# Sums at the chunks' ends: a product with ones in place of stores and loads, in a Mamba and FFN block on one core

## The chip, the cores and the metric

The kernel runs on one core of a Trainium2 chip. The metric is the device time of one execution in microseconds. TensorE (PE) multiplies matrices into PSUM, VectorE (DVE), ScalarE (ACT) and GpSimd (POOL) work elementwise, and SyncE (SP) issues nearly all DMAs. Each engine runs its own queue in order and waits for the others by semaphores.

## The reference

There are 4 sequences of 512 tokens with 256 features. A small modulation gives shifts, scales and gates `sa, ca, ga, sb, cb, gb` for each sequence. Then:

```python
h = _layernorm(x) * (1 + ca) + sa
x = x + ga * attn(h)          # Mamba-like, below
h = _layernorm(x) * (1 + cb) + sb
x = x + gb * ffn(h)           # silu(h W1) * (h W3), Hadamard transform, W2

# attn, with 32 heads of 8 channels and 64 states
xBC, z, A_log = split(u @ W_in.T)
x, Bm, Cm = split(depthwise_conv4(xBC) + conv_b)
a  = -softplus(A_log)                    # one decay a head and token
Lm = exp(segsum(a))                      # decay from token s to token l
M  = einsum('blhn,bshn,bhls->bhls', Cm, Bm, Lm)
y  = einsum('bhls,bshp->blhp', M, x) + D * x
out = (y * silu(z + z_bias)) @ W_out.T
```

The kernel cuts the 512 tokens into 8 chunks of 64 (`Q = 64`, `NC = 8`). Inside a chunk it computes M directly. Between chunks it carries a state for each head; the state is multiplied by the decay of a whole chunk, which is the Exp of the running sum of `a` at the chunk's end. This factor, for each head and chunk, is what the change is about.

## The kernel before

The work is cut into 8 units: two halves `i` of the heads (16 heads each) by four sequences `b`, with all sequences of `i = 0` first. A unit has two quads `m` (index `pp`), and a quad has four steps `k` (pairs of heads), so there are 64 steps. After them come 32 steps of the FFN.

For each step, `project` (L780) makes the channels of B (`pbc`, then `bc`) and of C (`pcc`, then `cc`) by six TensorE products each, and `conv` (L722) finishes them on ACT, DVE and POOL. `prep_l` (L773) makes the decays `l` inside the chunks from a product `pl` whose operands `dl` and `dr` are loaded by `load_d`. `attend` (L790) makes the products `pG` for two steps and multiplies them by `l` on DVE. `turn_b` (L807) transposes `bc`.

For each quad, `states` (L870) makes the chunks' states (`ps`, copied to `st`), `turn_states` (L896) transposes them (`sT`) and runs the scan over the chunks (`sn`) with the factors `dc`, and `inter` (L910) and `intra` (L882) make the outputs `pi` and `py`.

For each sequence, `prologue` (L663) has five parts: layer norm, modulation (`ht`, spilled to DRAM as `htd`), running sums of the decays (parts `p` and full sums `phs`, stored to DRAM as `pd`), the decays to the chunks' ends (`df`), and their transpose (`pw`, `wds`). In `phs` a partition is 32t + h for the quarter t of the tokens and the head h, and the free dimension holds the quarter's 128 tokens, so two chunks' ends. `write_sums` (L717) stores the ends to DRAM as `pend`, in four DMAs. For each unit `x_fetch` (L815) loads `pd` as `ex` and `pend` as `de` (spread over all 128 partitions), and `x_decays` (L827) takes the Exp of `ex`, the Exp of `de` into `dx`, sets the first chunk's factor to zero, and copies it into `dc` (1024 columns for both quads).

The order of the work is planned while the kernel is built. Each call has a time in steps for its writing (table `R`) and a due time in steps (table `T`). `Plan.schedule` (L266) goes through the engines with estimated durations. On an engine it takes, among the operations that it believes ready, the one with the earliest due time, but none whose due time is more than 10 steps after the earliest work left (`WINDOW`). For SP it keeps at most 8 DMAs under way. Buffers of one tag form a ring, ordered by due time, and a tile waits for the release of the tile that many buffers before it. The queues that come out of this are fixed: on the chip each engine waits at each instruction until its inputs are there.

The output weights are loaded in `load_wo` (L564), in two halves, through the ring `stage` of three buffers, which also serves `wm`, the modulation's weights (`load_mod`, L463; used by the products `pm` and `pg`), and projection weights `wq`. DVE scales each half of `wo` by 0.5:

```python
sp.dma_start(st[:, :DM], wo_t[128 * k : 128 * k + 128])
ve.tensor_scalar(st[:, :DM], st[:, :DM], 0.5, None, ALU.mult)
```

Where TensorE would idle for over 300 ns by the plan, up to 60 products of zeros (`zeros<-idle`) fill the time. Nearly all instructions are issued by one line of the planner, L366, so the profile's groups are told apart by their tiles' names.

Of the kernel before, what the change touches and what calls it, by code (L numbers as in the profile page):

```python
# [366 lines left out]


def mamba_ffn(tc, ctx, u, c_t, wmod, win_t, cw, cb, zb, dsk, wo_t, w13_t, w2_t,
              k_ident, k_reset, k_dl, k_dr, k_had, k_own, out):  # L370
    nc = tc.nc
    plan = Plan(slack=SLACK, retile=RETILE, window=WINDOW)
    ve, ac, gp, pe, sp = [Engine(plan, n, e) for n, e in (("DVE", nc.vector), ("ACT", nc.scalar), ("POOL", nc.gpsimd),
# [42 lines left out]
    def cload(src, shape, name, eng=ac):  # L416
        t = const.tile(shape, F32, name=name)
        eng.dma_start(t, src)
        return t
# [22 lines left out]
    warm = const.tile([128, 4], F32, name="warm")  # L442
    ac.activation(warm, neghalf, AF.Tanh)

    idle = const.tile([128, S], BF16, name="idle")
    ve.memset(idle, 0.0)
    zeros = bank(ps_1, [128, S], "zeros", "y")
    for _ in range(FILLERS):
        plan.open = None
        pe.matmul(zeros, idle[:, :128], idle, start=True, stop=True, kind="b512").filler = True  # L450
    plan.open = None
    c_sb = cload(c_t.rearrange("(k p) b -> p k b", p=128), [128, 2, NB], "c_sb")

# [51 lines left out]
        return t  # L505

    wds = const.tile([128, NB, 4, 2, NH], F32, name="wds")
    hzb = const.tile([128, 2], F32, name="hzb")
    xpad = const.tile([128, 2, NC, 4, 32], F32, name="xpad")
    sts = [const.tile([128, NC - 1, 4, 32], F32, name=f"sts{pp}") for pp in range(2)]  # L510
# [3 lines left out]

    dls = [const.tile([94, 8, 128], BF16, name=f"dl{n}") for n in range(2)]
    drs = [const.tile([94, 4, S], BF16, name=f"dr{n}") for n in range(2)]
    kdl = const.tile([94, 128], BF16, name="kdl")
    kdr = const.tile([94, S], BF16, name="kdr")

    def spread_constants(n):  # L520
        ve.tensor_copy(dls[n], kdl.unsqueeze(1).to_broadcast([94, 8, 128]), kind=325)
# [134 lines left out]
        return ts  # L656

    ht, htd, h2d, x2d, ygd = {}, {}, {}, {}, {}
    wdec, p_dr, p_dr3, p_end = {}, {}, {}, {}

    xns, fulls, phss, dfs = {}, {}, {}, {}

    def prologue(b, part, fill=None):  # L663
        if part == 0:
            xns[b] = normalize(b, 0, x_in.pop(b))
        elif part == 1:
            fulls[b], ht[0, b] = modulate(b, 0, xns.pop(b))
            htd[b] = spill(f"htd{b}", ht[0, b])
        elif part == 2:

            full = fulls.pop(b)
            acc = mtile([128, 3, 128], f"pa{b}")
            pa, sums, rest = acc[:, 0], acc[:, 1], acc[:, 2]
            for k in range(2):
                for t in range(4):
                    pe.matmul(pa[32 * t : 32 * t + 32], wa[:, k], full[k][:, 128 * t : 128 * t + 128],
                              start=(k == 0), stop=(k == 1), skip_group_check=True, tile_position=(0, 32 * t), kind="sums")
            e = work([128, 128], f"spe{b}", "spe", 1)
            ac.activation(e, pa, AF.Abs)
            ac.activation(e, e, AF.Exp, scale=-1.0)  # L680
            ac.activation(e, e, AF.Ln, bias=1.0)
            if fill:
                fill()

            ve.scalar_tensor_tensor(pa, pa, 0.0, e, ALU.max, ALU.add)
            ve.tensor_tensor_scan(sums, reset, pa, 0.0, ALU.mult, ALU.subtract)

            parts = work([128, 3, 128], f"parts{b}", "parts", 1, BF16)
            ve.tensor_copy(parts[:, 0], sums)
            ve.tensor_tensor(rest, sums, parts[:, 0], ALU.subtract)  # L690
            ve.tensor_copy(parts[:, 1], rest)
            ve.tensor_tensor(parts[:, 2], rest, parts[:, 1], ALU.subtract)
            phs = phss[b] = work([128, 128], f"phs{b}", "phs", 1)
            ac.activation(phs, sums, AF.Copy)
            p_dr3[b] = dram.tile([NH, 3, S], BF16, name=f"p3{b}")
            p_dr[b] = dram.tile([NH, S], F32, name=f"pd{b}")
            p_end[b] = dram.tile([NH, NC], F32, name=f"pend{b}")
            sp.dma_start(p_dr3[b].rearrange("h r (t l) -> t h r l", t=4), parts, kind=3000)
            after(1, write_sums, b, phs)
        elif part == 3:  # L700

            phs = phss.pop(b)
            df = dfs[b] = work([128, 128], f"df{b}", "df", 1)
            p_c = phs.rearrange("p (c l) -> p c l", l=Q)
            ve.tensor_tensor(df.rearrange("p (c l) -> p c l", l=Q), p_c[:, :, Q - 1 :].to_broadcast([128, 2, Q]),
                             p_c, ALU.subtract, kind=727)
            ac.activation(df, df, AF.Exp)
        else:
            pw = mtile([128, 128], f"pw{b}")
            pe.transpose(pw, dfs.pop(b), ident, kind="turn")  # L710

            wdec[b] = wds[:, b]
            for q in range(2):
                ac.activation(wdec[b][:, :, q], pw.rearrange("p (t h) -> p t h", h=NH), AF.Copy,
                              scale=own[:, 0, 8 * q : 8 * q + 1])

    def write_sums(b, phs):  # L717
        sp.dma_start(p_dr[b].rearrange("h (t l) -> t h l", t=4), phs, kind=4300)
        for t in range(4):
            sp.dma_start(p_end[b][:, 2 * t : 2 * t + 2], phs[32 * t : 32 * t + 32, Q - 1 :: Q], kind=5800)  # L720

    def conv(ps, tl, dst):  # L722
        w = cw_sb[:, tl]
# [21 lines left out]
        one0=-11.83, one1=-7.06, one2=-4.93, one3=-4.48, one4=-3.88,  # L745
    )
    T = dict(
        attend=0.36, turn_b=0.36, prep_l=-0.51, proj_b=-0.63, proj_c=-0.8, load_d=-6.56, states=0.1, intra=0.9,
        turn=2.34, inter=2.64, x_proj=2.37, x0=4.16, x1=8.55, x2=4.65, x3=3.51, gate_z=6.56, fin0=3.05, fin1=4.05,
        fin2=4.15, fin3=6.83, pro0=-9.52, pro1=-6.69, pro2=-4.23, pro3=1.75, pro4=0.64, next_ht=-6.78, pro04=1.42,  # L750
        quads=0.78, xz1=32.52, wo=21.57, mod=20.38, w2=38.38, wf0=61.86, wf1=70.35, wf2=67.94, load_w2=63.65,
        first_h2=59.92, lag=10.06, next_h2=-8.14, load_x=-11.25, spread=1.25, up=3.02, load_out=4.89, out=18.28,
        one0=-9.5, one1=-7.21, one2=-5.05, one3=-1.53, one4=-0.3,
    )

    def where(k):
        i, b = units[k // 8]
        return i, b, (k // 4) % 2, k % 4

    lts, bcs, ccs, bts, exs, des, xcs, xds, dcs, stt, pys, zts = ({} for _ in range(12))  # L760

    def load_d(m):

# [51 lines left out]
    def x_fetch(n):  # L815
        i, b = units[n]
        exs[n] = work([128, S], f"ex{n}", "ex")
        sp.dma_start(exs[n], p_dr[b].apply(lambda r: bass.AP(r.tensor, r.offset + 16 * i * S, [[S, 16], [0, 8], [1, S]]), [128, S]), kind=3600)

        des[n] = work([128, 16, NC], f"de{n}", "de", 1)  # L820
        sp.dma_start(des[n], p_end[b].apply(lambda r: bass.AP(r.tensor, r.offset + 16 * i * NC,
                                                              [[0, 128], [NC, 16], [1, NC]]), [128, 16, NC]), kind=3800)

    def x_part1(n):
        x_decays(n)

    def x_decays(n):  # L827
        ex = exs[n]
        ac.activation(ex, ex, AF.Exp)

        de = work([128, 16, NC], f"dx{n}", "dx", 1)
        ac.activation(de.rearrange("p (a g j) c -> p a g (j c)", a=2, g=4),
                      des.pop(n).rearrange("p (g a j) c -> p a g (j c)", a=2, g=4), AF.Exp)
        ac.activation(de[:, :, 0:1], de[:, :, 0:1], AF.Copy, scale=0.0)
        dc = dcs[n] = work([128, 16, HD, NC], f"dc{n}", "dc", 1)
        ac.activation(dc, de.unsqueeze(2).to_broadcast([128, 16, HD, NC]), AF.Copy)

    def x_proj(n):
        i, b = units[n]
# [30 lines left out]
    def states(m):  # L870
# [8 lines left out]
        stt[m] = work([128, 4, 128], f"st{m}", "st", 1)  # L879
        ac.activation(stt[m], pst, AF.Copy)  # L880

    def intra(m):  # L882
        n, pp = divmod(m, 2)
        if pp == 0:
            pys[n] = bank(ps_1, [128, S], f"py{n}", "y"), bank(ps_1, [128, S], f"pi{n}", "yi")
        py = pys[n][0]
        for c in range(NC):
            for g in range(4):
                l = slice(Q * c, Q * c + Q)
                pe.matmul(py[32 * g : 32 * g + 32, l], xpad[:, pp, c, g], lts[4 * m + g][:, l],  # L890
                          start=(pp == 0 and c == 0), stop=(pp == 1), skip_group_check=True,
                          tile_position=(0, 32 * g), kind="outs")
        for g in range(4):
            lts.pop(4 * m + g)

    def turn_states(m):  # L896
# [3 lines left out]
        for t in range(4):  # L900
            pe.transpose(pt[:, :, :, 2 * t : 2 * t + 2].rearrange("p g (h x) q -> p (g h) q x", h=2), st[:, t], ident, kind="turn")
        sn = work([128, 4, 16, NC], f"sn{m}", "xd", 2)
        ve.tensor_tensor_scan(sn.rearrange("p g x c -> p (g x c)"),
                              dcs[n][:, 8 * pp : 8 * pp + 8].rearrange("p h x c -> p (h x c)"),
                              pt.rearrange("p g x c -> p (g x c)"), 0.0, ALU.mult, ALU.add)
        o = 16 * pp
        gp.tensor_tensor(sts[pp][:, :, :, o : o + 16].rearrange("p c g x -> p g x c"), sn[:, :, :, : NC - 1],
# [95 lines left out]
    zb_sb = cload(zb, [128, 2], "zb_sb", sp)  # L1003
    d_sb = cload(dsk, [128, 2], "d_sb", sp)
    own = cload(k_own, [128, 4, 16], "own", sp)
    q11 = fetch_quad(1, 1)
    had = cload(k_had, [128, 128], "had", sp)
    prologue(0, 0)
# [165 lines left out]
def _constants():  # L1174
# [12 lines left out]
    while had.shape[0] < 128:  # L1187
        had = np.block([[had, had], [had, -had]])

    own = (p // 64)[:, None, None] ^ (np.arange(4) % 2)[None, :, None] == (np.arange(16) // 8)[None, None, :]  # L1190
    return dict(k_own=own.astype(np.float32), k_ident=np.eye(128, dtype=np.float32), k_reset=reset, k_dl=dl, k_dr=dr,
                k_had=(had / 64.0).astype(np.float32))


# [41 lines left out]
```

## Time and profile before

| what | value |
|---|---|
| median of 3 runs | 553.67 us (551.88 to 554.48) |
| profiled execution, own time | 557.63 us |
| its span, first to last instruction | 555.8 us |
| mean granted TensorE clock | 0.99 |
| busy: PE, DVE, ACT, POOL | 535.1, 403.2, 386.8, 328.2 us |
| DMAs of the chunks' ends | 16 stores `pend` (0.2 KB each), 8 loads `de` (64 KB each) |
| `dx<-de` Exp, 128 columns | 8 x 335 ns |
| `dx<-dx` zeroing, 16 columns | 8 x 246 ns |
| `dc<-dx` copy, 1024 columns | 8 x 1075 ns |

The profile is one execution on the hardware. PE is TensorE's products and PEld its weight loads, which overlap them. Products are pipelined and their ends are modelled, so a busy PE is not one at its peak. The granted clock is the share of full speed that TensorE got. In a list of waits "A <- B: 5.4, 2, 4.0" means that A stood idle for B, 5.4 us in total, twice, at most 4.0 us. In the chain of waits each line is a start time, a length and what the chain passed through. An f32 product that isn't in the rounded format `fp32r` shows as two records.

### The profile page before, as it was taken

The numbers are of one execution on the slowest core, as the hardware profiler recorded it, in microseconds if no ns is written. First come the engines' busy times: TensorE is split into PE (matmuls) and PEld (weight loads), VectorE is DVE, ScalarE is ACT, GpSimd is POOL, SyncE is SP. The second block draws the span as 40 slices with busy tenths as digits, with TensorE's granted clock in tenths as the row PEclk, the third lists the DMA queues.
The fourth block names the chain that finished last, engine by engine and source line by source line (L and its number), as shares of the span: only waits on it lengthen the run. The fifth ranks groups of instructions, "written<-read, shape, count | busy, mean of one in ns | idle before, by whom it ended". The sixth has DMA issues, their size and how long they took to land.

```text
span 555.8 us, 16369 instructions
## 1 busy us (share of the span) xinstructions
PE 535.1 (96%) x6885; PEld 427.4 (77%) x6890; DVE 403.2 (73%) x672; ACT 386.8 (70%) x666; POOL 328.2 (59%) x299
## 2 busy tenths in 40 slices
PE   8899999979998999999999999999989999999996
PEld 4666787758776777777787778777868888888886
DVE  6969889957965988896799989878955533324332
ACT  3999899958987899887787896889763333233231
POOL 7774458435734697663587657758966444425243
PEclk8999999989998999999999999999999999999999
DMA  8532201233125234311022803361391240502002
GB/s 233 173 92 68 71 30 50 70 101 111 43 44 165 66 99 126 106 59 18 20 66 66 267 16 78 147 208 40 118 325 63 89 149 4 158 1 85 1 26 88
DMA packets 41792, 51.99 MB, mean 94 GB/s; under 512 B 17942, under 2 KB 29940, under 8 KB 41720
## 3 DMA queue, kind: packets, MB, share of 16 engines
q1 hardware_dynamic: 41448, 50.96, 29.5%
q8 instruction: 54, 0.88, 0.7%
q14 instruction: 18, 0.15, 0.1%
q10 hardware_dynamic: 272, 0.00, 0.0%
HBM read 33.51 MB, written 17.44 MB: 92 GB/s over the span
## 4 chain that ended last, share of the span: by engine, by line
PE 69%; DVE 14%; DMA 7%; ACT 7%; issue 3%; SPq 1%; POOL 0%; ACTq 0%; DVEq 0%; POOLq 0%
PE f L366 16%; PE pbc L366 11%; PE pcc L366 11%; PE pG L366 4%; PE pdy L366 4%; PE pdyi L366 4%; PE bT L366 4%; PE ps L366 2%; DVE bc L366 2%; DMA wo<-wo_t 2%; PE py L366 2%; DVE cc L366 2%; PE pi L366 2%; PE pl L366 2%; PE px L366 2%
## 5 line engine op out<-in xcount | busy, mean ns | idle before, releaser
L366 DVE SCALAR_TENSOR_TENSOR bc<-pbc,cw_sb,bc 128x511 f32<-128x511 f32 (+1 forms) x128 | 95.0, 743 | 19.3 <-ACT cv L366 17.4
L366 DVE SCALAR_TENSOR_TENSOR cc<-pcc,cw_sb,cc 128x511 f32<-128x511 f32 (+1 forms) x128 | 95.0, 742 | 13.4 <-ACT cv L366 11.4
L366 POOL TENSOR_TENSOR cc<-cc,cv 128x509 f32<-128x509 f32 x64 | 69.7, 1088 | 52.2 <-DVE cc L366 38.3
L366 POOL TENSOR_TENSOR bc<-bc,cv 128x509 f32<-128x509 f32 x64 | 71.2, 1112 | 45.2 <-DVE bc L366 23.6
L366 PE MATMUL f<-h,wf 128*128 128x512 f32 x384 | 93.8, 393 | 0.0
L366 PEld LDWEIGHTS f<-h,wf 128*128 128x128 f32 x384 | 69.9, 188 | 13.7 <-issue 0.2
L366 POOL TENSOR_TENSOR fl<-ft,fh 128x512 fp32r<-128x512 f32 x31 | 39.9, 1288 | 61.4 <-ACT fh L366 61.2
L366 DVE SCALAR_TENSOR_TENSOR ft<-ft,f 128x512 f32<-128x512 f32 x32 | 21.9, 686 | 62.7 <-ACT ft L366 62.7
L366 ACT ACTIVATE bc<-pbc,cb_sb,cw_sb 128x512 f32<-128x512 f32 x64 | 50.4, 787 | 10.6 <-PE pbc L366 9.0
L366 ACT ACTIVATE cc<-pcc,cb_sb,cw_sb 128x512 f32<-128x512 f32 x64 | 50.5, 789 | 8.6 <-PE pcc L366 8.3
L366 ACT ACTIVATE fh<-ft 128x512 fp32r<-128x512 f32 x32 | 20.2, 631 | 51.4 <-PE pdyi L366 48.3
L366 PE MATMUL pbc<-ht,wq 128*128 128x512 f32 x192 | 53.0, 412 | 1.0 <-DVE cc L366 1.0
L366 PE MATMUL pcc<-ht,wq 128*128 128x512 f32 x192 | 52.5, 409 | 1.3 <-DVE bc L366 1.0
L366 PE MATMUL pcc<-hr,wq 128*128 128x512 f32 x192 | 52.8, 410 | 0.8 <-DVE bc L366 0.7
L366 PE MATMUL pbc<-hr,wq 128*128 128x512 f32 x192 | 52.2, 407 | 0.0
L366 ACT ACTIVATE bt<-bT 128x512 f32<-128x512 f32 x64 | 38.8, 606 | 12.6 <-PE bT L366 12.6
L366 DVE TENSOR_TENSOR l<-pG,l 128x512 f32<-128x512 f32 x64 | 41.5, 682 | 7.8 <-PE pG L366 7.1
L366 PEld LDWEIGHTS pbc<-ht,wq 128*128 128x128 f32 x192 | 34.5, 189 | 15.9 <-ACT cc L366 4.0
L366 ACT ACTIVATE cv<-pbc,cw_sb 128x512 f32<-128x512 f32 x64 | 44.7, 698 | 1.5 <-PE pbc L366 1.1
L366 ACT ACTIVATE cv<-pcc,cw_sb 128x512 f32<-128x512 f32 x64 | 44.7, 699 | 0.3 <-PE pcc L366 0.3
L366 PEld LDWEIGHTS pcc<-ht,wq 128*128 128x128 f32 x192 | 34.6, 188 | 9.9 <-ACT wq L366 1.5
L366 PE MATMUL bT<-ident,bc 128*128 128x128 f32 x256 | 40.7, 281 | 1.3 <-ACT ht L366 0.6
(145 smaller groups left out, 1137.4 us busy)
## 6 DMA issues: line engine op xcount, KB each, us to landing
wq<-win_t SPq DMA_DIRECT2D x16, 256.0 KB
htd<-ht SPq DMA_DIRECT2D x8, 512.0 KB
hr<-htd SPq DMA_DIRECT2D x8, 512.0 KB
h2d<-ht SPq DMA_DIRECT2D x8, 512.0 KB
h<-h2d SPq DMA_DIRECT2D x8, 512.0 KB
x<-u SPq DMA_DIRECT2D x7, 512.0 KB
ex<-pd SPq DMA_DIRECT2D x8, 256.0 KB
ygd<-yg SPq DMA_DIRECT2D x4, 512.0 KB
```

The costliest lines, as they stand in the source:

```text
L366: getattr(o.engine.real, method)(*map(real, args), **{k: real(v) for k, v in kw.items()})
```

## The change

The stores `pend` and the loads `de` are gone. In part 3 of `prologue` POOL multiplies the ends of `phs` by a constant mask `pick` into `ends`, which has 32 x 4 x 2 = 256 columns: for each head, each quarter and each of its two chunks there is one column, zero but in the one partition that holds that sum. TensorE multiplies `ends` by a 128x128 matrix of ones, so each of the 128 partitions gets all sums (`pn`). ACT takes the Exp of both halves of the heads, one into a buffer `de` for the unit `i = 0`, one into the constant tile `dec` for `i = 1`, and sets the first chunk's factor to zero. The heads are put in order by the mask. The copy `dc` is made by each quad in `states`, with 512 columns, in place of one for each unit in `x_decays`.

Beside this, `idle` has 128 columns and the fillers read its first column repeatedly; `kdl` and `kdr` share a buffer of the ring `yg`; and all due times `T` are new. The table `R` is the same.

```diff
-    idle = const.tile([128, S], BF16, name="idle")
+    idle = const.tile([128, 128], BF16, name="idle")
...
-        pe.matmul(zeros, idle[:, :128], idle, start=True, stop=True, kind="b512").filler = True
+        pe.matmul(zeros, idle, idle[:, :1].to_broadcast([128, S]), start=True, stop=True, kind="b512").filler = True
...
+    dec = const.tile([128, NB, 16, NC], F32, name="dec")
+    ones = const.tile([128, 128], F32, name="ones")
+    gp.memset(ones, 1.0)
...
-    kdl = const.tile([94, 128], BF16, name="kdl")
-    kdr = const.tile([94, S], BF16, name="kdr")
+    kd = work([94, 128 + S], "kd", "yg", 1, BF16)
+    kdl, kdr = kd[:, :128], kd[:, 128:]
...
-            p_end[b] = dram.tile([NH, NC], F32, name=f"pend{b}")
...
             ac.activation(df, df, AF.Exp)
+
+            ends = work([128, 32, 4, 2], f"en{b}", "ends", 1)
+            gp.tensor_tensor(ends, pick.unsqueeze(3).to_broadcast([128, 32, 4, 2]),
+                             p_c[:, :, Q - 1].unsqueeze(1).unsqueeze(1).to_broadcast([128, 32, 4, 2]), ALU.mult)
+            pn = mtile([128, 32, 8], f"pn{b}")
+            pe.matmul(pn, ones, ends.rearrange("p m t q -> p m (t q)"), start=True, stop=True, kind="gate")
+            for i in range(2):
+                d = dea[i, b] = dec[:, b] if i else work([128, 16, NC], f"de{b}", "de")
+                ac.activation(d, pn[:, 16 * i : 16 * i + 16], AF.Exp)
+                ac.activation(d[:, :, 0:1], d[:, :, 0:1], AF.Copy, scale=0.0)
...
         sp.dma_start(p_dr[b].rearrange("h (t l) -> t h l", t=4), phs, kind=4300)
-        for t in range(4):
-            sp.dma_start(p_end[b][:, 2 * t : 2 * t + 2], phs[32 * t : 32 * t + 32, Q - 1 :: Q], kind=5800)
...
     T = dict(
-        attend=0.36, turn_b=0.36, prep_l=-0.51, proj_b=-0.63, proj_c=-0.8, load_d=-6.56, states=0.1, intra=0.9,
-        turn=2.34, inter=2.64, x_proj=2.37, x0=4.16, x1=8.55, x2=4.65, x3=3.51, gate_z=6.56, fin0=3.05, fin1=4.05,
-        fin2=4.15, fin3=6.83, pro0=-9.52, pro1=-6.69, pro2=-4.23, pro3=1.75, pro4=0.64, next_ht=-6.78, pro04=1.42,
-        quads=0.78, xz1=32.52, wo=21.57, mod=20.38, w2=38.38, wf0=61.86, wf1=70.35, wf2=67.94, load_w2=63.65,
-        first_h2=59.92, lag=10.06, next_h2=-8.14, load_x=-11.25, spread=1.25, up=3.02, load_out=4.89, out=18.28,
-        one0=-9.5, one1=-7.21, one2=-5.05, one3=-1.53, one4=-0.3,
+        attend=0.32, turn_b=0.44, prep_l=-0.48, proj_b=-0.53, proj_c=-0.94, load_d=-5.82, states=0.2, intra=0.97,
+        turn=2.11, inter=2.32, x_proj=2.63, x0=3.34, x1=9.64, x2=2.66, x3=3.55, gate_z=6.9, fin0=3.24, fin1=3.64,
+        fin2=3.85, fin3=7.01, pro0=-9.53, pro1=-8.16, pro2=-4.2, pro3=-1.53, pro4=1.54, next_ht=-7.04, pro04=1.83,
+        quads=-0.67, xz1=30.69, wo=18.7, mod=19.5, w2=38.55, wf0=56.92, wf1=67.73, wf2=63.44, load_w2=64.98,
+        first_h2=59.85, lag=6.12, next_h2=-5.77, load_x=-6.16, spread=5.23, up=2.87, load_out=11.33, out=15.94,
+        one0=-7.18, one1=-6.04, one2=-4.13, one3=0.26, one4=-0.05,
     )
...
-        des[n] = work([128, 16, NC], f"de{n}", "de", 1)
-        sp.dma_start(des[n], p_end[b].apply(lambda r: bass.AP(r.tensor, r.offset + 16 * i * NC,
-                                                              [[0, 128], [NC, 16], [1, NC]]), [128, 16, NC]), kind=3800)
...
         ac.activation(ex, ex, AF.Exp)
-
-        de = work([128, 16, NC], f"dx{n}", "dx", 1)
-        ac.activation(de.rearrange("p (a g j) c -> p a g (j c)", a=2, g=4),
-                      des.pop(n).rearrange("p (g a j) c -> p a g (j c)", a=2, g=4), AF.Exp)
-        ac.activation(de[:, :, 0:1], de[:, :, 0:1], AF.Copy, scale=0.0)
-        dc = dcs[n] = work([128, 16, HD, NC], f"dc{n}", "dc", 1)
-        ac.activation(dc, de.unsqueeze(2).to_broadcast([128, 16, HD, NC]), AF.Copy)
...
         ac.activation(stt[m], pst, AF.Copy)
+
+        i, b = units[m // 2]
+        dcs[m] = work([128, 8, HD, NC], f"dc{m}", "dc", 1)
+        ac.activation(dcs[m], dea[i, b][:, 8 * pp : 8 * pp + 8].unsqueeze(2).to_broadcast([128, 8, HD, NC]), AF.Copy)
...
-                              dcs[n][:, 8 * pp : 8 * pp + 8].rearrange("p h x c -> p (h x c)"),
+        ve.tensor_tensor_scan(sn.rearrange("p g x c -> p (g x c)"), dcs.pop(m).rearrange("p h x c -> p (h x c)"),
...
+    pick = const.tile([128, 32, 4], BF16, name="pick")
+    sp.dma_start(pick, k_pick)
...
+    m = np.arange(32)
+    head = 16 * (m // 16) + 4 * (m // 2 % 4) + 2 * (m // 8 % 2) + m % 2
+    pick = (p % 32)[:, None, None] == head[None, :, None]
+    pick = pick & ((p // 32)[:, None, None] == np.arange(4)[None, None, :])
```

More of the change, by code (lines that the diff above doesn't have):

```diff
@@ L369, in mamba_ffn @@
 def mamba_ffn(tc, ctx, u, c_t, wmod, win_t, cw, cb, zb, dsk, wo_t, w13_t, w2_t,
-              k_ident, k_reset, k_dl, k_dr, k_had, k_own, out):
+              k_ident, k_reset, k_dl, k_dr, k_had, k_own, k_pick, out):
     nc = tc.nc
@@ L658, in mamba_ffn @@
     ht, htd, h2d, x2d, ygd = {}, {}, {}, {}, {}
-    wdec, p_dr, p_dr3, p_end = {}, {}, {}, {}
+    wdec, p_dr, p_dr3, dea = {}, {}, {}, {}
     xns, fulls, phss, dfs = {}, {}, {}, {}
@@ L758, in where @@
         return i, b, (k // 4) % 2, k % 4
-    lts, bcs, ccs, bts, exs, des, xcs, xds, dcs, stt, pys, zts = ({} for _ in range(12))
+    lts, bcs, ccs, bts, exs, xcs, xds, dcs, stt, pys, zts = ({} for _ in range(11))
     def load_d(m):
@@ L902, in turn_states @@
         sn = work([128, 4, 16, NC], f"sn{m}", "xd", 2)
-        ve.tensor_tensor_scan(sn.rearrange("p g x c -> p (g x c)"),
-                              dcs[n][:, 8 * pp : 8 * pp + 8].rearrange("p h x c -> p (h x c)"),
+        ve.tensor_tensor_scan(sn.rearrange("p g x c -> p (g x c)"), dcs.pop(m).rearrange("p h x c -> p (h x c)"),
                               pt.rearrange("p g x c -> p (g x c)"), 0.0, ALU.mult, ALU.add)
@@ L1190, in _constants @@
     own = (p // 64)[:, None, None] ^ (np.arange(4) % 2)[None, :, None] == (np.arange(16) // 8)[None, None, :]
-    return dict(k_own=own.astype(np.float32), k_ident=np.eye(128, dtype=np.float32), k_reset=reset, k_dl=dl, k_dr=dr,
+    m = np.arange(32)
+    head = 16 * (m // 16) + 4 * (m // 2 % 4) + 2 * (m // 8 % 2) + m % 2
+    pick = (p % 32)[:, None, None] == head[None, :, None]
+    pick = pick & ((p // 32)[:, None, None] == np.arange(4)[None, None, :])
+    return dict(k_pick=pick.astype(BF), k_own=own.astype(np.float32), k_ident=np.eye(128, dtype=np.float32), k_reset=reset, k_dl=dl, k_dr=dr,
                 k_had=(had / 64.0).astype(np.float32))
```

## The prediction

> **What bounds the kernel now.** First the page: busy shares and the granted clock.
>
> ```profile
> span 555.8 us, 16369 instructions
> PE 535.1 (96%) x6885; PEld 427.4 (77%) x6890; DVE 403.2 (73%) x672; ACT 386.8 (70%) x666; POOL 328.2 (59%) x299
> PEclk8999999989998999999999999999999999999999
> ```
>
> TensorE is the bound: 20.7 us of the span lie outside its busy time (555.8 - 535.1). So taking work off DVE, ACT, POOL or SP pays only where TensorE was made to wait, and work put onto TensorE is paid nearly in full. The clock row dips three times: at the start and in slices 9 and 13 (about 125 and 181 us, 13.9 us each). So next the table by stage around those two, in windows of 2 us (columns: window, length, PE, PEld, DVE, ACT, POOL busy with counts, granted clock, DMA share, GB/s).
>
> ```profile
> 114.00:116.00 2.00, 2.00 (x53) 1.76 (x43) 0.00 (x0) 0.00 (x0) 0.00 (x0) 1.00 0.84 267
> 116.00:118.00 2.00, 0.58 (x3) 0.25 (x2) 0.00 (x0) 1.22 (x3) 0.00 (x0) 1.00 0.71 215
> 118.00:120.00 2.00, 0.00 (x0) 0.00 (x0) 1.90 (x5) 2.00 (x6) 0.67 (x1) 1.00 0.41 143
> 120.00:122.00 2.00, 1.44 (x6) 1.24 (x6) 1.96 (x4) 1.26 (x3) 1.14 (x2) 0.92 0.00 0
> 122.00:124.00 2.00, 2.00 (x30) 1.26 (x33) 1.95 (x3) 1.36 (x3) 1.09 (x1) 0.50 0.03 8
> 124.00:126.00 2.00, 2.00 (x78) 1.88 (x71) 0.87 (x2) 0.74 (x2) 1.08 (x1) 0.72 0.00 0
> ```
>
> At 114 to 116 DVE, ACT and POOL all stand still; at 116 to 122 TensorE loses 1.42 + 2.00 + 0.56 = 3.98 us; then it works at a clock of 0.92, 0.50 and 0.72, which costs another 2 x (0.08 + 0.50 + 0.28) = 1.72 us. The same figure comes back at 169 to 177: 1.19 + 0.56 = 1.75 us of idle time, then clocks of 0.97, 0.50 and 0.67, worth 1.72 us. Together 9.2 us. The chain of waits says who did it, and the list of waits gives the sizes.
>
> ```profile
> 104.05 6.97 DMA pend<-phs
> 111.03 7.04 DMA wo<-wo_t
> ...
> 156.97 5.47 DMA pd<-phs
> ...
> 163.09 5.61 DMA wo<-wo_t
> ```
>
> ```profile
> POOL wo L366 <- DVE wo L366: 11.9, 2, 7.2
> DVE wo L366 <- DMA wo<-wo_t: 9.7, 2, 5.4
> PE pl L366 <- DVE l L366: 5.4, 2, 4.0
> ACT ex L366 <- DMA ex<-pd: 4.1, 1, 4.1
> ```
>
> Both times DVE stands at the scaling of a `wo` half (L568) whose load was issued late: at 111.03, after SP had waited for a slot behind the `pend` stores, and at 163.09, behind an `ex` load that had to wait for `pd`. Everything queued behind it on DVE, the `l` product that the next `pl` needs among it, waits too. In the first case ACT also stood 4.1 us at `ex`.
>
> **Removed.** 16 stores `pend` and 8 loads `de`. By the timeline of SP four stores take 1.74 to 1.90 us to issue and a load 0.32 to 0.40, so 4 x 1.85 + 8 x 0.35 = 10.2 us of SP's time; SP isn't the bound. Directly they gain little: nobody but two weight loads waits for `de` (0.6 us), and at the first stall the load `ex` ahead of `wo` in SP's queue (109.74) waits for `pd` anyway, so with the queue in the same order `wo` would go out hardly earlier. At the start the four stores lie between `pd` (22.66) and `dl` (25.42), and TensorE waits for `dl` and `dr` until 32.72; but ACT is busy throughout 22 to 50 us there, so I take 0, with 0 to 1.9 us of gain as bounds.
>
> The Trainium skill, in "DMA: Bandwidth & Descriptors" (Rules for kernel authors), speaks against the change: issue a transfer early and wait late, and its fixed cost is covered. By that rule alone the removal would gain 0 and the additions below would make the kernel slower by 3.2 us; the 9.7 us of DVE's wait above show a neighbour's transfer that is not covered.
>
> **Moved: the due times, which I count as the main effect.** SP takes a load up to 10 steps ahead of the earliest work left. `wo` moves from 21.57 to 18.70, the modulation weights `wm3`, `wm4` from 20.38 to 19.50. A step is (408.97 - 38.84) / 62 = 5.97 us, from the first and the last `pG` group, two steps each. So `wo` comes 2.87 x 5.97 = 17 us earlier: from 111 to about 94 us, where SP issues nothing but one `ygd` between 84.7 and 102, and ahead of the prologue's stores at 102. And the order in the ring of three `stage` buffers turns round: `wo` now stands before `wm3` and `wm4`, so its second half needn't wait for the buffer that `pm` frees at 163; both halves find free ones. Also `x1` (the Exp of `ex`) goes from 8.55 to 9.64 and `x0` (its load) from 4.16 to 3.34: 1.9 steps or 11 us more between load and use, against a wait of 4.1 us. What is late next is the planner's belief in a short landing: `wo` took 7.0 and 5.6 us in a busy queue; the shortest landing bounded in the trace is `p`, at most 3.4 us (156.19 to 159.61). I leave 0.75 us of stall for each half (bounds 0 and 4), so 9.2 - 1.5 = 7.7 us are won.
>
> The price of the half clock is read from these rows: 1.72 us after an idle time of 3.98 and as much after 1.75. The page "TensorE: Matmul & The Clock Gate" (HAM oscillation) names idle gaps over about 3.4 us as what drops the clock; by it the second stall would have had no such price, and 7.5 us in all would be to win; the second dip in the trace differs.
>
> **Added on TensorE.** Four products of f32 ones with 256 columns. Nearest is the gate product, f32 and 256 columns wide:
>
> ```profile
> 183.78 1.82 PE pg L366 x8
> ```
>
> Eight records are four products, 0.455 us each; so 4 x 0.455 = 1.82 us, in full on the path (bounds: 0.43 by half of `hd`, 2 x 0.605 / 2 = 0.605, so 1.7 to 2.4).
>
> **Added on POOL.** Four products of 128x256, nearest `w2b` on POOL at 0.759 us, and one memset (844 ns for 896 columns, so about 0.12 for 128): 3.2 us. POOL's in-order queue has the conv's last additions (`bc`, `cc`) behind it; at 59% it covers that. TensorE's in-order queue has the projections behind `pn`. The nearest such waits, of a weight load for POOL, are 0.4 us (`pi` for `sts`) to 0.8 (`bT` for `ht`), partly covered by the products still running; I take 4 x 0.2 = 0.8 us (bounds 0 and 4 x 2). The result is needed five steps later, some 30 us, by the `dc` of `states`, so nothing waits for the Exp itself.
>
> **ACT.** Eight Exp of 128 columns out of PSUM (near `spe<-pa`, 296 ns) for eight out of SBUF (335), and the eight zeroings stay: -0.3 us. The copies `dc` become 16 x about 0.66 (`yg`, 663 ns for 512) = 10.6 us for 8.6, so +2.0 us. ACT has idle time in the middle (13 to 14 of 15 us busy) but none at 22 to 50 us, where the chain runs over it: two Exp and two zeroings, 2 x (0.30 + 0.25) = 1.1, and half a `dc`, 0.66, take the place of 0.40 + 0.27 + 1.06. Net about 0, but the first half `dc` may queue before `st`; I take +0.6 us (bounds 0 and 2).
>
> **At no cost.** The load of `pick` (one issue, 0.43 us, ahead of `q11`, whose split comes 12 us later); the smaller `idle` and its broadcast (fillers run only where TensorE would idle); `kdl` and `kdr` in the buffer of `yg`, first written at step 11 (the second spreading, due at 5.23, is over by then; else `gate_y` waits for one copy of 1.2 us). In the FFN TensorE is fully busy from 420 to 550 us, so `lag`, `up` and `out` only reorder it; `lag` from 10.06 to 6.12 leaves about four down-products after the last up-product, 4 x 1.4 = 5.6 us of cover for a tail of some 2.5 (0.60 + 2 x 0.69 + 0.63).
>
> **Sum.** -7.7 + 1.8 + 0.8 + 0.6 = -4.5 us. The profiled execution took 557.63 us (555.8 of span and 1.8 around it), 4 us over the median of 553.67. I apply the difference to the median: 549.2 us. Changes under 0.5%, 2.8 us, can't be told from none here. The forecast's own range: from all of the 9.2 won and no waits (-9.2 + 1.8 + 0.4 = -7, 546.7) to a threshold gain (550.9).
>
> **Rivals.**
> - *All waits go.* The `ps` wait of 1.9 us at 414 (DMA share 1.0 there) goes too, since `wf0` loads 4.94 steps earlier, and 1 to 2 us are won at the start: -9.2 + 2.4 - 1.9 - 1.5 = -10.2, so 543.5. For it: all loads spread out. Against: DVE is 93 to 99% busy at 90 to 105 and 285 to 300 us, which no edit touches.
> - *The wait moves.* SP's order changes, but `ex` still waits for `pd`, and DVE, ACT or TensorE (`pm` for `wm`) stand at another load: half of the 9.2 us stays and 3.2 us are added: -4.6 + 3.2 = -1.4, so 552.3. The stores were then never what mattered.
> - *Slower: TensorE waits for POOL.* `pn` stands in TensorE's queue behind phs, POOL's queue and the masked product. If POOL is late by 2 us or more, that idle time drops the clock as 1.75 us did, at 1.72 us each: three prologues in the full stretch cost 3 x (2 + 1.7) = 11.1 us. With 7.7 won and 2.4 added: +5.8, so 559.5; at half the prologues 556. It decides from about 1.5 us of wait each. Against: POOL is at 4.9 to 9.8 of 15 us in those stretches.
>
> **Chances.** Forecast 0.42, all waits go 0.18, the wait moves 0.18, slower 0.22. So faster 0.60, same 0.18, slower 0.22. The range from 543.5 to 557.0 leaves out the outer part of the first and last rivals.
>
> **What would show it.** Right: no `pend` or `de` among the issues; `pn` eight records at 0.38 us; `wo` issued before 102 us in both halves; DVE's wait for `wo` under 2 us instead of 9.7; no clock of 0.50 after 100 us; TensorE's idle time near 15 us instead of 20.7. Wrong: a wait of TensorE for `ends` or of ACT for `pn`, the clock at 0.50 elsewhere, or the same two stalls still there with another name.

## The result, and the profile after

The changed kernel takes 544.57 us (median of 6 runs, 543.80 to 547.38) against 554.17 us of the kernel before in the same set (6 runs): a ratio of 0.9836, 95% interval 0.9802 to 0.9870, or 9.6 us faster. A second set gave 0.9845 (0.9804 to 0.9885). The kernel before itself lay between 554 and 559 us in the sets that follow, so they are compared by their ratios to the kernel before in the same set. The profiled execution took 543.80 us, 542.0 of it the span, close to the median; that of before (557.63 us) had been 3.5 us over its own. By the ratio the gain is 9.1 us (7.2 to 11.0), a little less than by the medians.

The page of the changed kernel, its busy shares and the granted clock:

```profile
span 542.0 us, 16291 instructions
...
PE 529.2 (98%) x6884; PEld 425.6 (79%) x6887; DVE 404.5 (75%) x672; ACT 386.6 (71%) x674; POOL 328.8 (61%) x304
...
PEclk8999999999999999999999999999999999999999
```

TensorE's time outside its busy time is 542.0 - 529.2 = 12.8 us, where it was 20.7, and both dips of the clock after 100 us are gone. The windows in which three engines stood still before (same columns as in the prediction):

```profile
114.00:116.00 2.00, 2.00 (x41) 1.74 (x31) 2.00 (x4) 1.34 (x3) 1.08 (x1) 1.00 0.13 49
116.00:118.00 2.00, 2.00 (x14) 1.59 (x13) 1.20 (x2) 1.55 (x3) 0.62 (x1) 1.00 0.00 0
118.00:120.00 2.00, 2.00 (x57) 1.56 (x59) 1.58 (x3) 2.00 (x4) 1.15 (x2) 1.00 0.03 8
120.00:122.00 2.00, 2.00 (x67) 1.78 (x56) 1.96 (x4) 2.00 (x5) 1.23 (x2) 1.00 0.29 117
```

TensorE is busy throughout at the full clock. SP's timeline shows both halves of `wo` going out at 75.5 us, not at 111 and 163, and the wait of DVE for `wo` (9.7 us) and of ACT for `ex` (4.1 us) are no longer in the list of waits:

```profile
75.53 1.25 SPq L366 DMA_DIRECT2D wo<-wo_t  x2
76.82 12.92 SPq L366 DMA_DIRECT2D wm<-wmod  x2
```

The added work, in the list of groups by shape (busy us, mean ns, idle time before it):

```profile
L366 ACT ACTIVATE dc<-de 128x512 f32<-128x512 f32 x8 | 5.5, 693 | 0.0
...
L366 ACT ACTIVATE dc<-dec 128x512 f32<-128x512 f32 x8 | 5.2, 652 | 0.4 <-DVE sn L366 0.4
...
L366 POOL TENSOR_TENSOR en<-pick,phs 128x256 f32<-128x256 bf16 x4 | 2.6, 660 | 1.4 <-ACT phs L366 1.4
...
L366 PE MATMUL pn<-en,ones 128*128 128x256 f32 x8 | 2.4, 379 | 0.0
```

The products have the records of the gate product (379 ns), and TensorE never waits for them or for POOL's mask. One thing in SP's timeline had not been looked at in the prediction: how long `ex`, which reads what `pd` stored, has to wait for it. Before, for the second sequence:

```profile
52.29 0.72 SPq L366 DMA_DIRECT2D pd<-phs  x1
53.06 1.89 SPq L366 DMA_DIRECT2D pend<-phs  x4
55.05 0.34 SPq L366 DMA_DIRECT2D dl<-p  x1
55.48 0.30 SPq L366 DMA_DIRECT2D dr<-p  x1
57.88 0.58 SPq L366 DMA_DIRECT2D ex<-pd  x1
```

and after:

```profile
57.09 0.70 SPq L366 DMA_DIRECT2D pd<-phs  x1
59.55 0.32 SPq L366 DMA_DIRECT2D dl<-p  x1
59.96 0.31 SPq L366 DMA_DIRECT2D dr<-p  x1
60.36 0.58 SPq L366 DMA_DIRECT2D ex<-pd  x1
```

From `pd` to `ex` it took 5.59 us before and 3.27 after. SP was through with `dr` at 55.78 and stood 2.1 us for `pd` to land. For the four sequences the figures are 5.71, 5.59, 7.06, 5.49 before and 3.95, 3.27, 4.08, 3.24 after. SP's own list of waits before has the wait in all four:

```profile
SPq L366 <- DMA pd<-phs: 7.6, 4, 2.3
```

After, the list has no wait for `pd`, so there the times are only upper bounds of its landing. The stores `pend` come behind `pd`, and yet `pd` lands later with them; that they are the cause is tested below. The plan believes in 4.3 us for `pd`.

### The profile page after: what moved, and what is told of

Same layout as the page of the kernel before. It is cut to its first block, busy times and chain, and to the rows that moved or that the text cites. A ratio compares the mean times of both kernels' runs of the same rounds, so it can differ in the third digit from the quotient of the medians.

```text
span 542.0 us, 16291 instructions
## 1 busy us (share of the span) xinstructions
PE 529.2 (98%) x6884; PEld 425.6 (79%) x6887; DVE 404.5 (75%) x672; ACT 386.6 (71%) x674; POOL 328.8 (61%) x304
## 4 chain that ended last, share of the span: by engine, by line
PE 71%; ACT 11%; DVE 11%; issue 2%; POOL 2%; DMA 2%; SPq 0%; POOLq 0%; DVEq 0%; ACTq 0%
PE f L366 16%; PE pbc L366 11%; PE pcc L366 11%; PE pdy L366 4%; PE bT L366 4%; PE pdyi L366 4%; PE pG L366 4%; ACT cv L366 2%; PE ps L366 2%; PE py L366 2%; DVE cc L366 2%; PE pi L366 2%; DVE bc L366 2%; PE pl L366 2%; PE po L366 2%
## 5 line engine op out<-in xcount | busy, mean ns | idle before, releaser
L366 POOL TENSOR_TENSOR bc<-bc,cv 128x509 f32<-128x509 f32 x64 | 70.1, 1095 | 50.7 <-DVE bc L366 23.3
L366 ACT ACTIVATE ft<-f 128x512 f32<-128x512 f32 x32 | 19.2, 598 | 36.0 <-PE f L366 36.0
```

The lines of the kernel that those rows point to most:

```text
L366: getattr(o.engine.real, method)(*map(real, args), **{k: real(v) for k, v in kw.items()})
```

## The experiments

Two theories stood against each other: the due times win the time (the prediction), or the stores do, since what lands beside them lands late. Twelve runs in three sets tell them apart.

**The two halves of the change.** First the new due times alone on the kernel before:

> The kernel before (stores and loads of the chunks' ends kept), with the new due times alone. If the due times make the gain (the prediction's theory), it is as fast as the changed kernel or some 2 to 3 us faster, since the four products with ones are not paid: 541 to 546 us, and no clock of 0.50 after 100 us. If the gain is that of the removed stores and loads, it stays at 551 to 556 us, with DVE waiting for wo again.

Measured: 548.87 against 557.99 us, ratio 0.9815 (0.9763 to 0.9866). `wo` goes out at 76.3 us and no engine waits for it, though `pd` to `ex` still takes 4.8 to 6.0 us. Then the changed kernel with the table `T` of before:

> The changed kernel with the old due times. If the due times make the gain, the additions are all that is left: 554 to 558 us, with the wo load still issued behind ex and DVE waiting 4 to 10 us for it. If the removed stores make the gain, 543 to 547 us.

Measured: 550.62 us, ratio 0.9866 (0.9820 to 0.9911). The first theory had expected 554 to 558 and DVE waiting for `wo`; but `pd` to `ex` is 3.87, 3.13, 4.21 and 3.29 us, and though `wo` goes out as late as 109.1 and 156.1 us, DVE doesn't wait for it. Each half alone gives nearly the whole gain: 1.8% and 1.3%, and 1.6% together. Both cure the waits of DVE for `wo` and of ACT for `ex`.

The half clock is another matter. In this run TensorE is idle for 0.4 us in all from 150 to 162 us, and the clock drops all the same:

```profile
162.00:164.00 2.00, 2.00 (x76) 1.80 (x64) 0.75 (x1) 0.78 (x1) 0.00 (x0) 0.50 0.51 150
164.00:166.00 2.00, 2.00 (x16) 1.77 (x9) 1.80 (x5) 0.60 (x1) 0.11 (x1) 0.66 0.87 204
```

That is again 1.7 us, as after each of the two stalls.

**Only the due times of `wo`.** In the kernel before:

```diff
-        quads=0.78, xz1=32.52, wo=21.57, mod=20.38, ...
+        quads=0.78, xz1=32.52, wo=18.7, mod=19.5, ...
```

> The kernel before with only two due times moved, wo from 21.57 to 18.7 and mod from 20.38 to 19.5. If the two stalls at wo are the step that counts, 7 to 9 us are won: 545 to 547 us, and DVE's wait for wo falls from 9.7 us to under 2. If the gain is spread over all due times, or the stores make the next load late in its turn, 550 to 555 us.

Measured: 555.36 us, ratio 0.9937 (0.9907 to 0.9967), 3.5 us. The wait for `wo` is gone, but the chain of waits around the prologues, which showed `wo` before, now has others in its place:

```profile
113.74 6.43 DMA de<-pend
...
154.85 5.31 DMA pd<-phs
...
160.17 6.52 DMA ex<-pd
```

The list of waits has 3.6 us of ACT for `ex` and 1.1 for `de`. From 166 to 172 us TensorE loses 2.5 us, and from 170 to 178 the clock is at 0.50 to 0.77: a stall is paid here at another load. With `x0` and `x1` moved as well:

```diff
-        ... x0=4.16, x1=8.55, ... wo=21.57, mod=20.38, ...
+        ... x0=3.34, x1=9.64, ... wo=18.7, mod=19.5, ...
```

> The kernel before with four due times of the new ones: wo and mod, and x0 and x1 (the load of ex and its use). With wo alone moved the wait went over to ex and the ratio was 0.994. If these two waits are all that the new due times cure, the ratio is that of all new due times, 0.977 to 0.987. If the other due times matter as much, it stays at 0.990 to 0.996.

Measured: 551.76 against 559.34 us, ratio 0.9880 (0.9837 to 0.9923). The clock doesn't dip after 100 us. Four of the due times give 1.2% of the 1.8% that all of them give; the intervals overlap, so what the others add isn't settled.

**`wo` back to its late place** in the changed kernel:

```diff
-        quads=-0.67, xz1=30.69, wo=18.7, mod=19.5, ...
+        quads=-0.67, xz1=30.69, wo=21.57, mod=20.38, ...
```

> The changed kernel with wo and mod set back to 21.57 and 20.38. If the two stalls at wo are the step that counts and come from these due times, they are back: 550 to 554 us, with clocks of 0.50 after 100 us. If the stores that are gone made wo late, the load lands in time all the same: 543 to 547 us.

> The changed kernel once more, beside the others of this set: ratio 0.980 to 0.987 to the kernel before. The time from the issue of pd to the issue of the ex that waits for it is 3.2 to 4.1 us, where it was 5.5 to 7.1 before.

> The changed kernel with wo and mod at 21.57 and 20.38, beside the changed kernel itself. If the due times of wo and mod matter once the stores are gone (the prediction's theory), it is 3 us or more slower than the changed kernel; if the landing is what matters, the two are within 2 us of each other.

Measured: 546.92 against 557.99 us in the first set, ratio 0.9790 (0.9745 to 0.9835); in the second 546.47 us, 0.9862 (0.9819 to 0.9904), beside the changed kernel's 545.40 us, 0.9845. The two can't be told apart. In the profile of the changed kernel's second set `pd` to `ex` is 3.2 to 4.1 us, as expected. With the late place SP issues `wo` at 106.6 and 151.3 us, long after the 75.5 of the changed kernel (before: 111.0 and 163.1), and DVE hardly waits for it:

```profile
DVE wo L366 <- DMA wo<-wo_t: 0.3, 1, 0.3
```

In the second run it is 0.7 us; before it was 9.7. Issued at 106.6, the first half is used at 110.24, so it landed within 3.7 us (4.0 in the second run), where the halves had taken 7.0 and 5.6. It also goes out earlier for its use: DVE came to it 3.4 us after the issue, where it had been 1.6 before. So without the stores, and with the other due times new, the place of `wo` doesn't matter, and the step that the prediction counted as the main effect isn't needed. The clock still drops once after 100 us in the first of these profiles, to 0.55 and 0.60 at 214 to 218, after 2.0 us of idle time; neither half of `wo` is near.

**The stores put back, alone.** In the kernel with the product and the old due times; nobody reads what they store:

```diff
+        for t in range(4):
+            sp.dma_start(p_end[b][:, 2 * t : 2 * t + 2], phs[32 * t : 32 * t + 32, Q - 1 :: Q], kind=5800)
```

> The kernel with the product and the old due times, and with the 16 stores of the chunks' ends put back, which nobody reads. If the stores lengthen the landing of pd and of the loads behind it, the time from pd to ex goes from 3.1 to 4.2 back to 5.5 to 7.1 us, DVE waits for wo again, and the ratio to the kernel before is 0.998 to 1.008 (all of the gain gone). If it was only the planner's other order, pd to ex stays at 3 to 4 us and the ratio near 0.987.

Measured: 556.96 against 554.57 us, ratio 1.0040 (1.0013 to 1.0066). All of the gain is gone, and `pd` to `ex` is 6.11, 5.55, 6.19 and 5.56 us again. SP's timeline at the third sequence, then from the lists of waits:

```profile
106.43 0.69 SPq L366 DMA_DIRECT2D pd<-phs  x1
107.56 1.74 SPq L366 DMA_DIRECT2D pend<-phs  x4
...
112.62 0.59 SPq L366 DMA_DIRECT2D ex<-pd  x1
...
113.90 0.46 SPq L366 DMA_DIRECT2D wo<-wo_t  x1
```

```profile
SPq L366 <- DMA pd<-phs: 7.6, 4, 2.2
DVE wo L366 <- DMA wo<-wo_t: 4.6, 1, 4.6
```

and what TensorE has from it, in the table by stage:

```profile
120.00:122.00 2.00, 0.33 (x2) 0.10 (x1) 0.96 (x3) 2.00 (x5) 0.00 (x0) 1.00 0.41 150
122.00:124.00 2.00, 0.49 (x3) 0.42 (x3) 2.00 (x5) 0.84 (x3) 1.72 (x2) 1.00 0.01 2
```

`wo`, out at 113.90, landed 7.1 us later, and TensorE lost 1.67 + 1.51 = 3.2 us: the first stall of the kernel before is back. The second isn't: that half has 7 us until its use. The profile shows no drop of the clock right behind the stall; it comes at 166 to 170 (0.57 and 0.58). What else makes up the loss wasn't followed.

**As many stores, but of long rows.** The same kernel, except that each store takes 32 rows of 512 bytes and not 64 elements of 4 bytes. TensorE's order of instructions is the same as in the last kernel, since the plan gives both stores the same cost:

```diff
-            sp.dma_start(p_end[b][:, 2 * t : 2 * t + 2], phs[32 * t : 32 * t + 32, Q - 1 :: Q], kind=5800)
+            sp.dma_start(p_end[b][:, 128 * t : 128 * t + 128], phs[32 * t : 32 * t + 32], kind=5800)
```

> As the kernel with the product, the old due times and the 16 stores, but each store takes 32 rows of 512 bytes in place of 64 single elements of 4 bytes; as many DMAs, TensorE's order is the same and the other queues' nearly. If the many single elements lengthen the landing, pd to ex falls from 5.5 to 6.2 us back to 3 to 4.5 and the ratio to 0.985 to 0.992. If it is the number of DMAs that SP issues and keeps under way, nothing changes: 5.5 us and a ratio of 1.000 to 1.007.

Measured: 552.23 against 559.34 us, ratio 0.9883 (0.9838 to 0.9928). SP's timeline at the same place:

```profile
104.72 0.69 SPq L366 DMA_DIRECT2D pd<-phs  x1
105.85 1.92 SPq L366 DMA_DIRECT2D pend<-phs  x4
...
109.11 0.58 SPq L366 DMA_DIRECT2D ex<-pd  x1
```

SP spends as long on the issues (1.92 and 1.74 us) and the stores move 64 times the bytes, yet `pd` to `ex` is 4.39 us here and 4.68, 3.49 and 3.53 for the others, SP doesn't wait for `pd`, and DVE doesn't wait for `wo`, which it uses 4.3 us after its issue (110.37 to 114.63) behind the same two loads. So neither SP's issue time nor the number of DMAs was the price: it is the form of the stores, 64 single elements each. Whether the number of pieces counts or their shortness isn't separated.

**One store of short rows, without the product.** The kernel before, with its old due times:

```diff
-        for t in range(4):
-            sp.dma_start(p_end[b][:, 2 * t : 2 * t + 2], phs[32 * t : 32 * t + 32, Q - 1 :: Q], kind=5800)
+        two = work([128, 2], f"two{b}", "two", 1)
+        ac.activation(two, phs.rearrange("p (c l) -> p c l", l=Q)[:, :, Q - 1], AF.Copy)
+        sp.dma_start(p_end[b].rearrange("h (t q) -> t h q", t=4), two, kind=5800)
```

> The kernel before with one store of the chunks' ends for each sequence in place of four: ACT first copies the ends side by side, so 128 runs of 8 bytes take the place of 256 of 4. No product, old due times. If the count of tiny elements sets the landing, pd to ex lies between, at 4.3 to 5.5 us, and the ratio at 0.990 to 0.998. If only no such store at all helps, 1.000; if the number of DMAs is what counts, 0.985 to 0.990.

Measured: 549.49 against 559.34 us, ratio 0.9827 (0.9787 to 0.9867): as much as the whole change, with an ACT copy of two columns in place of mask, product and Exp out of PSUM. It was more than expected. `pd` to `ex` is 6.21, 3.23, 5.64 and 3.11 us, short for two sequences of four. In the first the landing isn't the reason: there the store stands before `ex` in SP's queue, and SP's list of waits for that stretch has it waiting for ACT's copy:

```profile
SPq L366 <- ACT two L366: 1.7, 1, 1.7
```

In the third SP does wait 1.0 us for `pd`; why there and not in the second and fourth wasn't found. DVE waits 4.0 us for `wo` in two pieces, at most 2.7, and the clock doesn't dip.

**The loads put back, alone**, of half their size for want of space:

```diff
+        no = work([128, 8, NC], f"no{n}", "no", 1)
+        sp.dma_start(no, p_dr[b].apply(lambda r: bass.AP(r.tensor, r.offset + 16 * i * NC,
+                                                         [[0, 128], [NC, 8], [1, NC]]), [128, 8, NC]), kind=3800)
```

> The kernel with the product and the old due times, and with 8 loads spread to all partitions put back (256 bytes a partition in place of 512, out of pd, which nobody reads). If the stores alone are the cause, pd to ex stays at 3.1 to 4.2 us and the ratio at 0.985 to 0.990. If the loads take a part, the ratio is 0.992 or more.

Measured: 551.29 against 554.57 us, ratio 0.9943 (0.9917 to 0.9969), against 0.9866 (0.9820 to 0.9911) without them. `pd` to `ex` stays at 3.1 to 4.6 us, so the loads don't act through that landing, and DVE doesn't wait for `wo`. TensorE waits 1.3 us for `wm` in its profile, but so it does in the runs with new due times that gain 1.8% and 1.2% (1.6 and 1.5 us). The two intervals come from different sets and all but touch, while the medians differ by 0.7 us (551.29 and 550.62). So whether the loads take a part isn't settled; in the same set the stores cost more by 5.7 us.

**The price of the product.** The changed kernel, with each of its four products made five times:

> The changed kernel with each of the four products with ones made five times, so 16 more at 0.455 us = 7.3 us of TensorE. If TensorE's time is paid in full, 7 to 8 us more than the changed kernel, a ratio near 0.998 to the kernel before; if idle time hides half of it, near 0.991; if all, 0.984.

Measured: 552.97 against 559.34 us, ratio 0.9892 (0.9859 to 0.9925). Its group and its page:

```profile
L366 PE MATMUL pn<-en,ones 128*128 128x256 f32 x40 | 9.4, 382 | 0.0
```

```profile
PE 538.6 (98%) x6921; PEld 433.0 (79%) x6925; DVE 403.3 (73%) x672; ACT 387.4 (70%) x674; POOL 328.4 (60%) x304
```

By the ratios it is 0.0047 to 0.0056 slower than the changed kernel, 2.6 to 3.1 us; by its own medians 7.6 us (552.97 - 545.40), but the kernel before was 4.8 us slower in that set too. TensorE's busy time is up by 9.4 us, of which 7.0 are the products. So the 16 added products cost between 2.6 and 7.6 us, and the four of the change between 0.7 and 1.9. Whether idle time hides a part is not settled.

No version clearly beats the changed kernel: the ratios of the new due times alone (0.9815), of the one store (0.9827) and of `wo` set back (0.9790 and 0.9862) have intervals that overlap its own.

## Why the prediction was right, and where its reasons were wrong

The sign and the range held (549.2 forecast, 543.5 to 557.0; 544.57 measured), but the gain is 9.6 us and not 4.5, and one step gave a wrong cause.

- *What bounds the kernel* held for the idle time: two waits at `wo` made it. The runs in which these waits and that for `ex` are gone, or under 1 us, gain 1.1 to 2.1%, but for the one with the loads put back (0.6%); the run that brings the first of them back loses everything. That these waits also made the half clock isn't shown: both dips went with them in the changed kernel, but a dip of the same 1.7 us comes at 162 to 166 us with the product alone, where no stall stands before it. Nor does each execution of the kernel before show the same dips: its mean clock lay between 0.982 and 1.000.
- *"Directly they gain little"*, of the removed stores, is the step that failed in the argument. It counted SP's issue time (10.2 us, rightly worthless) and argued that `ex`, ahead of `wo` in the queue, waits for `pd` "anyway". That wait for `pd` was itself the work of the stores: 5.5 to 7.1 us with them, 3.1 to 4.2 without. That `wo` "would go out hardly earlier" was true of the first half (109.1 for 111.0 us with the product alone), but without the stores it also landed sooner. The row was there to read: SP idle from 55.78 to 57.88 before `ex`. With the old due times removal and product together win 7.5 us (0.9866), so the removal wins more than that; only beside the new due times is its 0 about right.
- *"The due times, which I count as the main effect"*: half right. They are enough alone, 0.9815, but so is the removal, 0.9866, and `wo` back in its old place changes nothing measurable. So the time would have fallen into the range even with `wo` late (546.92 and 546.47 us), the step that the forecast mainly rests on; in that the agreement is luck. Of the due times those of `ex` count as well as those of `wo`: with `wo` alone the wait moved to `ex` and `de`, as the rival "the wait moves" had it; only that rival's conclusion, that the stores never mattered, fell. `wo` was expected at about 94 us and came at 75.5. (The last `pG` group begins at 408.90 us, not 408.97; the step stays 5.97.)
- *The 9.2 us at the two stalls, 7.7 of them won*: by the two profiles all of it was won, and more. Of 13.8 us between the two spans, 7.9 are idle time and 5.9 busy time. In the busy time, 3.4 are the two dips; the fillers fell by 2.4 (15.6 to 13.2 us, 49 records to 40), as much as the products' records added; 2.5 us were not followed further. Between the medians it is 9.6, because the profiled execution of before lay 3.5 us over its median.
- *Added on TensorE, 1.82 us*: the records agree with the gate product's to the nanosecond; on the path between 0.7 and 1.9 us, by the run with five products.
- *Added on POOL and ACT, 1.4 us on the path*: too much for POOL, whose product took 0.660 us and not 0.759; TensorE waited for it not at all, so the slower rival had no ground. (That rival's "at half the prologues 556" doesn't come out of its terms either: 5.55 - 7.7 + 2.4 gives 553.9.) What ACT's part cost on the path no run shows; the start didn't suffer, since the first `pG` group came at 35.61 us, where it was 38.84, and ACT's copies took 652 to 693 ns, as estimated.
- *What would show it*: the `wo` issues, the waits and the clock came as said; idle time fell to 12.8 us rather than 15.

So the sum was too small by about five microseconds, and not through the 0 for the stores. By the run with the new due times alone these win 10.3 us (7.5 to 13.2) where 7.7 were counted, and removal and additions on top of them cost 1.2 to 1.7 where 3.2 were counted (0.9815 against 0.9836 and 0.9845). Both differences lie within the noise, so the shortfall can't be divided more sharply. With the changed kernel alone the prediction would have looked confirmed, for the due times did move `wo`. The runs that undo one half showed that the other half does it too.

## What to carry to other kernels

Price a DMA by what it does to the landing of its neighbours, not only by its issue time and its bytes: read how long SP stands before a load that depends on a store, and compare it with a place without the suspect between them. Gathering stores of single elements into longer runs is worth trying before anything else is rebuilt; here a copy of two columns did as much as the product. Where queues are fixed in advance from believed durations, a transfer that lands 2 us late can stall engines far from it (here TensorE, through DVE's queue). A shorter landing and an earlier issue or later use each cured it here, so their gains didn't add up.

## What the runs showed of the hardware

Four stores of 64 elements of 4 bytes, 1 KB together, lengthen the landing of a 64 KB store issued before them: SP waits 1.3 to 2.2 us for it at each of the four sequences in the run with the stores put back, and not at all in the one with rows of 512 bytes in place of the elements, in which TensorE's order is the same. A 128 KB load behind the elements landed 7.1 us after its issue, and behind the rows within 4.3.

And DVE was held up by POOL. Its scaling of `wo` and the cast after it (128x256 f32) take 0.28 to 0.30 us. In fourteen places in these runs one of them began while an operation ran on POOL that had 0.18 us or more to go; each of the fourteen ended 0.14 to 0.16 us after that operation, and took 0.33 to 1.18 us. In the changed kernel the scaling that began at 85.61 us ended at 86.64, and POOL's addition ran from 85.40 to 86.49. That wasn't followed with a run of its own.
